# Expert blocks of the first four rows split off, and state-space fronts issued beside the other blocks

## The chip, the cores and the metric

The kernel runs on one core of one Trainium2 chip. The metric is the device time of one launch in microseconds (us). Before the change it is 3760.65 us, the median of three runs (3760.41 to 3761.23). Engines are named as in the profile: PE (TensorE matmul), PEld (TensorE weight load), DVE (VectorE), ACT (ScalarE), POOL (GpSimd) and SP (SyncE, which only issues DMAs here).

## The reference

The input x has 32 rows of 256 tokens of 128 floats. Two layers follow each other; each has a mixer and a feed-forward part, each with shift, scale and gate vectors per row from a modulation matmul. Layer 0 mixes by 16-head attention with rotary positions, then routes each token to two of eight gated experts. Layer 1 mixes by a state-space scan in both directions, followed by a sine and cosine expansion, and ends with capacity-limited experts. The change touches the experts of layer 0 and the start of the state-space part. Cut to these:

```python
# layer 0, experts: top-2 of 8, for every token of every row
logits = x @ gate_w
mult, sel = _sparse_mixer_routing(logits)              # two experts and their factors
w = jnp.sum(mult[:, :, None] * (sel[:, :, None] == jnp.arange(E)[None, None, :]), axis=1)
h = jax.nn.silu(jnp.einsum('th,ehf->etf', x, w1)) * jnp.einsum('th,ehf->etf', x, w3)
out = jnp.einsum('etf,efh,te->th', h, w2, w)
# layer 1, state space, for every row
xz = jnp.einsum('ble,ie->bli', x, in_w)
xc, z = jnp.split(xz, 2, axis=-1)
xc = _silu(conv(xc, conv_w) + conv_b)                  # 4 taps along the tokens
dt, Bm, Cm = jnp.split(jnp.einsum('bld,rd->blr', xc, xproj_w), [DTR, DTR + DS], axis=-1)
dt = jax.nn.softplus(jnp.einsum('blr,dr->bld', dt, dt_w) + dt_b)
h = dA_t * h + dBx_t                                   # scan over the tokens
```

## The kernel before, in words

The stages run one behind the other: modulation, attention, expert blocks of layer 0, state-space stage, experts of layer 1.

**Attention and routing.** Attention takes row after row in an order written out by hand (`with tc.manual_schedule`, L651): the engines PE, ACT, DVE and POOL execute what the loop issues, in that order. Behind attention, `routed` (L314) routes finished rows in chunks (`CHUNKS`, six of four rows, four of two). It normalizes and modulates the rows into h (L327 and L328 are its two POOL multiplications), multiplies by the gate, finds the two experts and their factors with small DVE operations, counts where each token stands in its expert's room (`filled` keeps the counts over chunks), and scatters each 128-token tile twice into `rows_in` by an indirect DMA on POOL (`scattered`, L276, issue at L280). `rows_in` has a room for all tokens per expert, plus one block; before the first scatter `blanked` (L242) fills it with blank rows, in four parts from a tile of 16 rows a partition, at rows 2 to 5 of attention. The last chunk (rows 30 and 31) is finished only when attention is, so its routing stands alone behind it (L781).

**Block table and blocks.** From `filled`, DVE works out for each block which expert and which rows it has (L785 to L822): blocks hold 256 rows of one expert, so 2·8192/256 + 8 − 1 = 71 blocks are enough for every split of the tokens. The loop at L826 then makes for each block: an indirect gather of the expert's weights (L830; skipped by an index out of bounds if its buffer, of three, has them already), an indirect gather of 256 rows (L839, five buffers), the cast of their targets (to_u, L847, DVE), two transposes (L850, PE, into PSUM of two buffers) and their copy (L852, DVE), the matmuls pa and pb in two halves (L861), Silu (L862, ACT), the product g (L863, DVE), the matmuls po (L869, eight of 128 columns for each token tile), the scaling (L877, ACT) and two scatters into `rows_out` (L280, POOL). Here no order is written out: a list scheduler orders the instructions by their dependences, and can move those of other parts ahead, as it does with the taps multiplication of `weights_kept` (L690, called at block 17, L828; its POOL operation is L700), the loads of the state-space weights.

**State-space stage.** Again an order by hand (L1347), in units g; a row has 16 of them (`UNITS`). Its `front` (L1005) is cut into 22 steps at the slots of `FRONT_AT`, from 39 units ahead of the row's first scan pass to 5 ahead. The front loads the row's two expert outputs (of_two, L1012, SP) and vectors gb and mod (L1014, L1016), adds them into x on POOL (L1018 to L1020), normalizes (L296 to L308: statistics on DVE, rstd on POOL, ACT), modulates (L1024, L1025), normalizes again, transposes (L157), and makes in_w (L1039), conv (L1053, four groups of eight matmuls), Silu (L1059), xp (L1069), the loads bc_d and bc (L1082), dt_w (L1096), Abs and Relu (L1103, L1104), Exp and Ln (L1106, L1107), and dt and u on POOL (L1109, L1111). All matmuls of fronts share one PSUM bank. ACT's function tables are loaded by hand in this stage (`table`, L990; load at L992). Each unit then has arg and ub matmuls (L1269), da (L1275, ACT), by_b (L1286, DVE), the scan (L1293, DVE), by_c (L1306, POOL) and gathered (L1325, PE). The loop starts at unit −39: row 0's front therefore runs ahead of the first scan, behind the last block.

Of the kernel before, what the change touches and what calls it, by code (L numbers as in the profile page):

```python
# [21 lines left out]
P = 128  # L22
# [47 lines left out]
def body(ctx: ExitStack, tc: tile.TileContext, a: dict, out: bass.AP):  # L70
# [155 lines left out]
    n_blocks = 2 * n_tok // BR + E - 1  # L226
# [11 lines left out]
    rows_out = scratch.tile([2 * n_tok, D], F32, tag="rows_out", name="rows_out")  # L238
    FILL = 16
    blank = rc.tile([P, FILL, WID], F32, tag="blank", name="blank")  # L240

    def blanked(part, parts):  # L242

        if part == 0:
            nc.gpsimd.memset(blank[:], 0.0)
            nc.gpsimd.memset(blank[:, :, D : D + 1], float(4 * n_tok))
        n = room // P // FILL // parts
        flat = rows_in[0:room, :].rearrange("(p a k) w -> p a (k w)", p=P, k=FILL)
        ins = nc.scalar.dma_start(
            flat[:, part * n : (part + 1) * n, :],  # L250
            blank[:].rearrange("p k w -> p (k w)").unsqueeze(1).to_broadcast([P, n, FILL * WID]),
        )
        blanks.append(ins.ins.name)
        if part == 0:
            nc.scalar.dma_start(rows_in[room:, :].rearrange("(p k) w -> p k w", k=2), blank[:, 0:2, :])
# [5 lines left out]
    nc.gpsimd.tensor_scalar(ids2[:], ids[:], float(n_tok), None, ALU.add)  # L261

    filled = rc.tile([P, E], F32, tag="filled", name="filled")
    nc.gpsimd.iota(
        filled[:], pattern=[[n_tok, E]], base=-1, channel_multiplier=0, allow_small_or_imprecise_dtypes=True
# [4 lines left out]
    groups = {"in": [], "out": []}  # L270
    sync = mybir.DependencyInfo(mybir.DependencyClass.Sync, mybir.DependencyReason.DATA)
    blanks = []
# [3 lines left out]
    def scattered(group, apart=False, **args):  # L276

        if apart:
            nc.gpsimd.memset(spacer[:], 0.0)
        ins = nc.gpsimd.indirect_dma_start(in_offset=None, **args).ins  # L280
        tc.declare_no_dep(ins, group=group, reason="rows of their own")
        tc.add_to_no_dep_group(group, ins)
        for b in blanks if group == "in" else ():
            tc.add_manual_dep(ins, b, sync, reason="blank rows first")
        groups[group].append(ins.name)
# [28 lines left out]
    def routed(first, n_rows, bank, apart):  # L314

        n = 2 * n_rows
        k = f"{n}_"
# [78 lines left out]
        for t in range(n):  # L396
            for row_u, h in zip(rows_at, hs):
                scattered(
                    "in",
                    apart,  # L400
                    out=rows_in[:],
# [4 lines left out]


    with ExitStack() as st:
# [8 lines left out]
        def a_bank():  # L417
            return ps_m.tile([P, 512], F32, tag="m", name="m")

# [231 lines left out]
        with tc.manual_schedule(engines=MANUAL):  # L651
            for s in range(-2 * UNITS_A - PREPARED, n_s + 9 * UNITS_A):
# [18 lines left out]
                if i == 2 and b - 2 in range(4):  # L671
                    blanked(b - 2, 4)
                last = b >= n_b - 1
                if i == (0 if last else 2) and b - 1 in starts[1:-1]:
                    c = starts.index(b - 1) - 1
                    behind.append(routed(starts[c], CHUNKS[c], a_bank, True))
# [5 lines left out]
                if s > n_s + UNITS_A + 1 and not streams and not behind:  # L682
                    break
# [6 lines left out]
    def weights_kept():  # L690
# [50 lines left out]


        das = [wc.tile([P, 4 * T + 1], F32, tag=f"da{i}", name=f"da{i}") for i in range(3)]
        for t in das:
            nc.gpsimd.memset(t[:, :: T], 0.0)

        behind = wc.tile([4 * DS, 1], F32, tag="behind", name="behind")
        nc.vector.tensor_copy(behind[:], ident[: 4 * DS, DTR : DTR + 1])
# [11 lines left out]


    with ExitStack() as st:
# [3 lines left out]
        ps_m = pool(st, "b_psm", 2, PSUM)  # L766
# [9 lines left out]
        empty = bc.tile([P, E], F32, tag="empty", name="empty")  # L776
        nc.gpsimd.iota(
            empty[:], pattern=[[n_tok, E]], base=-1, channel_multiplier=0, allow_small_or_imprecise_dtypes=True
        )

        for _ in routed(starts[-2], CHUNKS[-1], lambda: ps_m.tile([P, 512], F32, tag="m", name="m"), False):  # L781
            pass


        restart("k")  # L785
        blocks = thin(bc, E)
        nc.vector.tensor_tensor(blocks[:], filled[:], empty[:], ALU.subtract)
        nc.vector.tensor_scalar(blocks[:], blocks[:], 1.0 / BR, 0.5 - 0.5 / BR, ALU.mult, ALU.add)
        nc.vector.tensor_scalar(blocks[:], blocks[:], ROUND, None, ALU.add)
        nc.vector.tensor_scalar(blocks[:], blocks[:], -ROUND, None, ALU.add)  # L790
        upto = thin(bc, E)
        nc.vector.tensor_tensor_scan(upto[:], ones[:, :E], blocks[:], 0.0, ALU.mult, ALU.add)
        past = wide(bc, n_blocks)
        nc.vector.tensor_tensor(
            past[:],
            iota_k[:].unsqueeze(2).to_broadcast([P, n_blocks, E]),
            upto[:].unsqueeze(1).to_broadcast([P, n_blocks, E]),
            ALU.is_ge,
        )
        of = thin(bc, n_blocks)  # L800
        nc.vector.tensor_reduce(of[:], past[:], AX.X, ALU.add)
        nc.vector.tensor_tensor(past[:], past[:], blocks[:].unsqueeze(1).to_broadcast([P, n_blocks, E]), ALU.mult)
        at = thin(bc, n_blocks)
        nc.vector.tensor_reduce(at[:], past[:], AX.X, ALU.add)
        nc.vector.tensor_tensor(at[:], iota_k[:], at[:], ALU.subtract)
        nc.vector.tensor_scalar(at[:], at[:], float(P), None, ALU.mult)

        nc.vector.scalar_tensor_tensor(at[:], of[:], float(n_tok // 2), at[:], ALU.mult, ALU.add)
        nc.vector.tensor_scalar(at[:], at[:], float(room // 2), iota_p[:], ALU.min, ALU.add)
        at_u = bc.tile([P, n_blocks], U32, tag="at_u", name="at_u")  # L810
        nc.vector.tensor_copy(at_u[:], at[:])

        nc.vector.tensor_scalar(of[:], of[:], float(E - 1), float(P), ALU.min, ALU.mult)
        w_at = thin(bc, n_blocks)
        nc.vector.tensor_scalar(w_at[:], of[:], iota_p[:], None, ALU.add)
        same = thin(bc, n_blocks)
        nc.vector.tensor_tensor(same[:, WBUF:], of[:, WBUF:], of[:, : n_blocks - WBUF], ALU.is_equal)
        nc.vector.scalar_tensor_tensor(
            w_at[:, WBUF:], same[:, WBUF:], float(2 * E * P), w_at[:, WBUF:], ALU.mult, ALU.add
        )  # L820
        w_u = bc.tile([P, n_blocks], U32, tag="w_u", name="w_u")
        nc.vector.tensor_copy(w_u[:], w_at[:])  # L822

        ws = [bc.tile([P, ROW], F32, tag=f"w{i}", name=f"w{i}") for i in range(WBUF)]
        two_rows = rows_in[:].rearrange("(r k) w -> r (k w)", k=2)
        for j in range(n_blocks):  # L826
            if j == n_blocks // 4:
                weights_kept()  # L828
# [13 lines left out]
                in_=two_rows,  # L842
                in_offset=bass.IndirectOffsetOnAxis(ap=at_u[:, j : j + 1], axis=0),
            )
            reads("in", got)
# [20 lines left out]
            for t in range(2):  # L866
                for c in range(NF):
# [11 lines left out]
                    "out",  # L879
                    out=rows_out[:],  # L880
                    out_offset=bass.IndirectOffsetOnAxis(ap=to_u[:, t : t + 1], axis=0),
                    in_=o[:, t, :],
                    bounds_check=2 * n_tok - 1,
                    oob_is_err=False,
                )
    layer0.close()
# [79 lines left out]
    with ExitStack() as st:  # L966
        sp = pool(st, "c_sp", 2)
        one = pool(st, "c_one", 1)
# [4 lines left out]
        ps_m = pool(st, "c_psm", 1, PSUM)  # L973


        y_bank = ps_y.tile([P, 2, T], F32, tag="y", name="y")
        m_bank = ps_m.tile([P, 2 * T], F32, tag="m", name="m")

        def bank():
            return m_bank  # L980

# [609 lines left out]
```

## Time and profile before

The profile is of one execution on the chip. Its own time is 32 us above the median of the runs; differences are taken within it.

| what | us |
|---|---|
| median of the runs | 3760.65 |
| profiled execution, its time | 3792.99 |
| profiled execution, its span | 3791.0 |
| last attention matmul (L632) starts | 870.49 |
| first block matmul pa (L861) starts | 921.11 |
| last block matmul group po (L869) starts | 1361.47 |
| first scan pass (L1293) starts | 1425.63 |
| PE busy in the span | 3141.5 (83%) |
| POOL busy in the span | 2678.0 (71%) |

How to read it: every line of the profile has a start, a length, an engine and a source line; brackets hold the time for which the engine stood idle ahead of it, and what ended that. PEclk is the TensorE clock that was granted. "out<-in" are the program's own names.

### The profile page before, as it was taken

What the parts mean: (1) busy time and instruction counts of PE and PEld (TensorE: products, weight loads), DVE (VectorE), ACT (ScalarE), POOL (GpSimd) and SP (SyncE); (2) the same over time, 40 slices, a digit from 0 to 9 for tenths busy, and PEclk for the clock granted to TensorE, in tenths of its full rate; (3) what the DMA queues carried; (4) which work ended last, traced back from release to release, by engine and by line L of the source; (5) the groups of instructions that cost most, each with busy time, mean ns of one, the idle gap of its engine ahead of it and who ended that gap; (6) DMA issues with size and microseconds to landing.
All of it is one profiled execution on the core that took longest, in us unless ns stands there. A gap on an engine that the chain in (4) does not pass through costs nothing.

```text
span 3791.0 us, 69007 instructions
## 1 busy us (share of the span) xinstructions
PE 3141.5 (83%) x27464; PEld 2150.3 (57%) x27464; DVE 2620.6 (69%) x3526; ACT 2340.3 (62%) x3402; POOL 2678.0 (71%) x2724
## 2 busy tenths in 40 slices
PE   6999999884999968888888888888888888788854
PEld 3655655553888845555555555555555555555543
DVE  3666666643233319988888988888988888988942
ACT  3666666551333325777777677777677777777751
POOL 4466666645666647887887887888888888888842
PEclk8999999986999978988988888889888889889966
DMA  2720000002222211111111111111111111111102
GB/s 78 285 113 27 24 27 25 28 18 83 92 85 87 82 34 30 28 32 36 32 32 36 32 33 37 32 34 35 32 33 37 32 37 32 32 39 26 29 17 72
DMA packets 149686, 183.27 MB, mean 48 GB/s; under 512 B 31263, under 2 KB 112950, under 8 KB 145140
## 3 DMA queue, kind: packets, MB, share of 16 engines
q1 hardware_dynamic: 121892, 97.72, 11.1%
q0 software_dynamic: 23168, 46.93, 3.9%
q10 hardware_dynamic: 4304, 34.21, 2.2%
q8 instruction: 215, 3.52, 0.4%
q14 instruction: 107, 0.88, 0.1%
HBM read 130.24 MB, written 86.41 MB: 57 GB/s over the span
## 4 chain that ended last, share of the span: by engine, by line
POOL 22%; PE 18%; ACT 9%; issue 7%; DVE 7%; ACTq 1%; DMA 1%; POOLq 0%; SPq 0%; DVEq 0%
POOL hs L1306 11%; PE m L1180 5%; PE arg L1269 4%; POOL r L1162 3%; DVE hs L1293 3%; ACT da L1275 3%; PE y L1325 3%; ACT L992 3%; DVE ub L1286 2%; PE m L1133 1%; PE ub L1269 1%; PE y L1314 1%; POOL rstd L303 1%; ACT mag L1171 1%; ACT r L1170 1%
## 5 line engine op out<-in xcount | busy, mean ns | idle before, releaser
L1306 POOL TENSOR_TENSOR hs<-hs,bc 128x1024 f32<-128x1024 f32 x512 | 1204.7, 2363 | 342.1 <-DVE hs L1293 322.6
L1293 DVE TENSOR_TENSOR_SCAN hs<-da,ub 128x1024 f32<-128x1024 f32 x512 | 1167.3, 2280 | 31.7 <-POOL u L1111 0.5
L1269 PE MATMUL arg<-dt,spread_a 32*128 32x256 f32 x4096 | 718.6, 447 | 95.4 <-ACT da L1275 91.4
L1275 ACT ACTIVATE da<-arg 128x1020 f32<-128x1020 f32 x512 | 521.5, 1019 | 345.1 <-PE ub L1269 286.0
L1269 PE MATMUL ub<-u,spread 32*128 32x256 f32 x4096 | 670.3, 445 | 41.9 <-DVE hs L1293 41.7
L1286 DVE TENSOR_TENSOR ub<-ub,bc 128x1024 f32<-128x1024 f32 x512 | 620.7, 1212 | 108.5 <-PE ub L1269 108.5
L1269 PEld LDWEIGHTS arg<-dt,spread_a 32*128 32x128 f32 x4096 | 432.1, 207 | 287.7 <-ACT da L1275 171.1
L576 DVE TENSOR_REDUCE q<-x 128x4 f32<-128x1024 f32 x256 | 312.8, 1222 | 214.2 <-PE x L569 199.6
L1269 PEld LDWEIGHTS ub<-u,spread 32*128 32x128 f32 x4096 | 410.1, 207 | 70.5 <-DVE hs L1293 64.4
L572 ACT ACTIVATE ex<-e 128x1024 f32<-128x1024 f32 x256 | 261.9, 1023 | 204.5 <-PE x L569 178.1
L569 PE MATMUL e<-qmT,kqT 32*128 32x256 f32 x2048 | 343.6, 415 | 52.5 <-ACT ex L572 52.1
L1325 PE MATMUL y<-hs,gather 128*32 128x256 f32 x4096 | 338.4, 456 | 0.8 <-POOL hs L1306 0.8
L992 ACT ACT_TABLE_LOAD x257 | 329.7, 1283 | 5.2 <-PEq L1575 0.7
L569 PE MATMUL x<-kqT 32*128 32x256 f32 x2048 | 305.0, 415 | 10.5 <-DVE q L576 10.5
L569 PEld LDWEIGHTS e<-qmT,kqT 32*128 32x128 f32 x2048 | 217.5, 191 | 111.1 <-ACT ex L572 83.9
L1053 PE MATMUL m<-oT,taps 128*128 128x256 f32 (+3 forms) x1024 | 261.9, 400 | 6.9 <-DVE tots L929 3.5
L1180 PE MATMUL m<-coef,mag 128*128 128x128 f32 x1024 | 225.3, 304 | 47.2 <-DVE h L1188 30.9
L1053 PEld LDWEIGHTS m<-oT,taps 128*128 128x128 f32 x1024 | 189.5, 195 | 78.4 <-issue 48.5
L1180 PEld LDWEIGHTS m<-coef,mag 128*128 128x128 f32 x1024 | 167.7, 206 | 104.6 <-DVE h L1188 43.5
L280 POOL DMA_INDIRECT rows_out<-o,to_u x142 | 144.3, 1016 | 114.3 <-ACT o L877 91.6
L863 DVE TENSOR_TENSOR g<-g,pb 128x512 f32<-128x512 f32 x142 | 97.6, 688 | 165.2 <-PE pb L861 153.3
L1325 PEld LDWEIGHTS y<-hs,gather 128*32 128x32 f32 x4096 | 121.1, 124 | 158.3 <-issue 112.1
(332 smaller groups left out, 6227.9 us busy)
## 6 DMA issues: line engine op xcount, KB each, us to landing
rows_in<-blank ACTq DMA_DIRECT2D x4, 8320.0 KB, 24.9
bc_d<-xd SPq DMA_DIRECT2D x64, 256.0 KB, 5.3
bc<-bc_d SPq DMA_DIRECT2D x32, 512.0 KB, 3.7
of_two<-rows_out SPq DMA_DIRECT2D x64, 128.0 KB, 2.6
mod_b<-mod SPq DMA_DIRECT2D x32, 256.0 KB, 4.0
mod<-mod SPq DMA_DIRECT2D x32, 192.0 KB, 3.2
x<-in_x SPq DMA_DIRECT2D x16, 256.0 KB, 5.5
mod<-mod SPq DMA_DIRECT2D x32, 128.0 KB, 3.0
```

The source lines that it names most:

```text
L569: nc.tensor.matmul(to, lhs, rhs, start=True, stop=True)
L572: nc.scalar.activation(ex[:], exs[k_e][:], AF.Exp, scale=1.0 / math.sqrt(DH))
L576: nc.vector.tensor_reduce(pad("q", b)[:, :, 2 * i : 2 * i + 2, DH].rearrange("p t h -> p h t"), found[:], AX.X, ALU.max, negate=True,)
L992: nc.scalar.preload_act_table_set(which)
L1053: nc.tensor.matmul(to, taps[:, d, n, c, :], of, start=(s == 0), stop=(c == 0), skip_group_check=True)
L1180: nc.tensor.matmul(ps[:, t * D : (t + 1) * D], turned[k // (GRID // 2)][1 - j][:, k % (GRID // 2), t * P : (t + 1) * P], coef[:, j, k, :], ...
L1269: nc.tensor.matmul(to, lhs, rhs, start=True, stop=True)
L1275: nc.scalar.activation(e.da.rearrange("p (g t) -> p g t", t=T)[:, :, inner], e.arg[:].rearrange("p i j t -> p (i j) t")[:, :, inner], AF.Exp,)
L1286: nc.vector.tensor_tensor(by_four, by_four, b_of, ALU.mult)
L1293: nc.vector.tensor_tensor_scan(e.hs[:].rearrange("p g t -> p (g t)")[:, ::step], e.da[:, ::step], e.ub[:].rearrange("p i j t -> p (i j t)" ...
L1306: nc.gpsimd.tensor_tensor(e.hs[:], e.hs[:], c_of, ALU.mult)
L1325: nc.tensor.matmul(y[r * RG : (r + 1) * RG, :], gather[:, q, :], of.hs[:, 2 * j + p, :], start=False, stop=(q == NQ - 1), skip_group_check ...
```

## The change

Rows 0 to 3 (the first chunk) get rooms, outputs, counts and blocks of their own: `early_in`, `early_out`, `early_filled`, and 2·1024/256 + 7 = 15 early blocks; the other 28 rows keep `rows_in` and `rows_out` with 2·7168/256 + 7 = 63 blocks. The early blocks come directly behind attention. The routing of the last chunk no longer stands ahead of all blocks: after each early block two of its steps are issued. The table of the later blocks comes behind the early ones. The transposes of the blocks have one PSUM buffer in place of two, because the fronts' bank is now reserved from the end of attention on.

The fronts are taken out of the state-space stage, with a pool of their own (`c_fp`). A class `Lead` keeps their slots; `ahead.step()` issues the front steps of one unit. It is called after each later block from the 15th on, and what is left follows the last block; units −39 to −3 are issued this way: all of row 0's front, twelve steps of row 1's and three of row 2's. They have the list scheduler's order, as the blocks around them, and `table` does nothing there, so loads of ACT's tables are put in by the compiler where functions change. The state-space loop starts at unit −2. The tiles da, with their memset (L745 before), are made at the start of the state-space stage instead of in `weights_kept`.

In attention, early blank rows are written at row 2 and the four parts for `rows_in` at rows 3 to 6, from a tile in attention's own pool; the loop no longer ends only when the routing in it has ended. The rest is renaming and pools.

```diff
-    n_blocks = 2 * n_tok // BR + E - 1
+    n_early = CHUNKS[0] * T
+    early_blocks = 2 * n_early // BR + E - 1
+    n_blocks = 2 * (n_tok - n_early) // BR + E - 1
...
-    def routed(first, n_rows, bank, apart):
+    def routed(first, n_rows, bank, apart, rh, rt):
         n = 2 * n_rows
+        group, to_rows, filled = ("in", rows_in, later_filled) if first else ("early_in", early_in, early_filled)
...
-                if s > n_s + UNITS_A + 1 and not streams and not behind:
+                if s > n_s + UNITS_A + 1 and not streams:
                     break
...
+    fp = state_space.enter_context(tc.tile_pool(name="c_fp", bufs=2, side="right"))
+    ps_s = state_space.enter_context(tc.tile_pool(name="c_pss", bufs=1, space=PSUM, side="right"))
+    m_bank = ps_s.tile([P, 2 * T], F32, tag="m", name="m")
...
+        group, outs = ("out", rows_out) if b >= CHUNKS[0] else ("early_out", early_out)
         for i in range(2):
-                of_i = rows_out[i * n_tok + b * T : i * n_tok + (b + 1) * T, :]
-                reads("out", nc.sync.dma_start(of_two[:, i], of_i.rearrange("(t p) d -> p t d", p=P)))
+            at = i * outs.shape[0] // 2 + b * T
+            of_i = outs[at : at + T, :]
+            reads(group, nc.sync.dma_start(of_two[:, i], of_i.rearrange("(t p) d -> p t d", p=P)))
...
+    class Lead:
+        def step(self):
+            if self.at >= -2:
+                return False
+            self.begin(self.at)
+            self.steps(self.at)
+            self.steps(self.at + 0.5)
+            self.at += 1
+            return True
+    ahead = Lead()
...
-        for _ in routed(starts[-2], CHUNKS[-1], lambda: ps_m.tile([P, 512], F32, tag="m", name="m"), False):
-            pass
...
-        for j in range(n_blocks):
-            if j == n_blocks // 4:
-                weights_kept()
+        assert early_blocks % WBUF == 0
+        behind.append(routed(starts[-2], CHUNKS[-1], routing_bank, False, rh, rt))
+        where = block_table("j", early_blocks, early_filled, n_early)
+        for j in range(early_blocks):
+            block(j, where, "early_", early_in, early_out)
+            if j == 2:
+                weights_kept()
+            for _ in range(2):
+                if behind and next(behind[0], behind) is behind:
+                    behind.pop(0)
+        for steps in behind:
+            for _ in steps:
+                pass
+        where = block_table("k", n_blocks, later_filled, n_tok)
+        for j in range(n_blocks):
+            block(j, where, "", rows_in, rows_out)
+            if j >= n_blocks // 4:
+                ahead.step()
+        while ahead.step():
+            pass
...
-            for g in range(FRONT_AT[0], n_u + 6 * UNITS):
+            for g in range(ahead.at, n_u + 6 * UNITS):
```

## The prediction

> **What bounds the kernel now.** The page's forty slices come first: they show which engine is full in which stage. A slice is 94.8 us; attention is slices 1 to 9, the expert blocks are the end of slice 10 to the middle of slice 15, the state-space stage follows.
>
> ```profile
> PE   6999999884999968888888888888888888788854
> DVE  3666666643233319988888988888988888988942
> POOL 4466666645666647887887887888888888888842
> PEclk8999999986999978988988888889888889889966
> ```
>
> The reader is to see PE at nine tenths through the blocks (slices 11 to 14), and two dips of PE and of its clock, at slices 9 to 10 and 15: the two seams that the change works on. The windows of 10 us open them. Columns: window, length, then busy time (and count) of PE, PEld, DVE, ACT, POOL, then granted clock, DMA share, GB/s. The first fence is the seam ahead of the blocks, with the first blocks behind it, the second that behind them.
>
> ```profile
> 900.00:910.00 10.00, 0.00 (x0) 0.00 (x0) 8.28 (x28) 0.00 (x0) 7.33 (x9) 0.50 0.13 40
> 910.00:920.00 10.00, 1.32 (x4) 0.58 (x4) 1.09 (x4) 0.00 (x0) 6.24 (x7) 0.50 0.36 113
> 920.00:930.00 10.00, 8.89 (x36) 7.55 (x37) 1.59 (x5) 2.16 (x4) 3.23 (x4) 0.71 0.58 204
> ```
>
> ```profile
> 1370.00:1380.00 10.00, 0.00 (x0) 0.00 (x0) 1.41 (x8) 0.88 (x2) 5.41 (x11) 0.50 0.35 87
> ```
>
> At the first seam DVE and POOL work in turn (block table, eight row scatters) and PE does nothing. At the second one row's front runs as a chain with one engine at a time. The timeline gives the ends (start, length, engine, line; in brackets the idle time before it and what ended it).
>
> ```profile
> 888.39 1.18 POOL L328 TENSOR_TENSOR h<-h,mod 128x512 f32<-128x512 f32 x1
> 913.19 1.00 POOL L839 DMA_INDIRECT h<-rows_in,at_u  x1 [2.15 <-DMA rows_in<-h,4_row]
> 921.11 2.04 PE L861 MATMUL pa<-hT,w 128*128 128x256 f32 x4 [2.59 <-issue]
> ```
>
> ```profile
> 1361.47 1.16 PE L869 MATMUL po<-w,g 128*128 128x128 f32 x8 [0.51 <-ACT o L877]
> 1363.31 0.98 POOL L280 DMA_INDIRECT rows_out<-o,to_u  x1 [0.63 <-ACT o L877]
> 1380.86 0.86 PE L157 MATMUL m<-ident,o 128*128 128x128 f32 x2 [18.23 <-ACT o L308]
> 1425.63 2.29 DVE L1293 TENSOR_TENSOR_SCAN hs<-da,ub 128x1024 f32<-128x1024 f32 x1
> ```
>
> So 71 blocks last from 921.11 to 1362.63, 441.5 us, **6.2 us a block** (6.15 between Silus), and from the last po to the first scan pass 63.0 us. Who limits a block is in the waits of 925 to 1362 (total, times, longest):
>
> ```profile
> DVE to_u L847 <- DMA h<-rows_in,at_u: 110.5, 53, 3.6
> POOL rows_out L280 <- ACT o L877: 91.0, 68, 6.2
> PE po L869 <- DVE g L863: 24.7, 28, 1.4
> ```
>
> PE waits only 24.7 us in 437: blocks are PE's. But POOL issues four indirect DMAs a block (two scatters, one weight and one row gather), each 1.0 long with 0.3 before it: 5.3 us of 6.15, so it has 0.85 us to spare. And DVE, which works in order, sits at to_u until the row gather has landed, while g, which PE waits for, stands behind it. In the periods I read to_u ended 0.3 to 1.4 us before its g could start. A POOL that falls further behind stops PE.
>
> **The change, part by part**, against the profiled run (3792.99 us, span 3791.0; that is 32.3 above the 3760.65 median, so I carry the difference, not the time, over to the median).
>
> *First seam, saved.* The first blocks need only the scatters of rows 0 to 3, done long before. In the changed order of POOL the first row gather follows the routing's second multiplication (L328, ends 889.57) directly. So it starts near 889.6, the first weight gather at 890.9; the weight of before was issued at 915.77 and its first pa came 5.34 later, so pa starts near 896.5: **24.6 us saved**. What could be late next is the taps multiplication (L700, 4.93 us on POOL), now behind the third row gather; it ends near 901.5, before block 0 has rows to scatter: no cost.
>
> *Seven more blocks.* 2·1024/256+7 = 15 early and 2·7168/256+7 = 63 later are 78, not 71. 7 × 6.15 = **43.1 us**, all on PE's path.
>
> *The last routing between early blocks.* Its eight scatters took 10.1 us (900.94 to 911.05); POOL now issues them in one run behind the first scatter of block 5, ahead of that block's weight gather, its second scatter and the row gather five blocks on. With some 2 us for the casts that they wait for (0.46 and 2.15 are the waits at the old place, so 0 to 4) POOL loses 12.4 less the 1.4 that to_u had: **11 us**; 0 if the queue had a block in hand, 14 with the longer wait. The small DVE operations (two routing and table stretches, 5.8 and 8.3 us of DVE before) now stand between g multiplications. DVE is busy 3 of 10 us there, so most are hidden: **3 us**, from 0 to 8. The idle PE that they filled is already in the first term.
>
> *Fronts beside the later blocks.* All of row 0's front, twelve steps of row 1's and three of row 2's are issued there, from later block 15 in the program. The scheduler puts their POOL operations in front, between later blocks 1 and 8: of_two, gb and x (3 × 0.72 a row, three rows), four sets of rstd (1.4 each) and two of h (1.44), 15 us, and 3.4 us for the gaps and a fifth set: 18.4 over five blocks with 0.85 to spare each is **13 us** (18.4 − 4.3 − 1). At their old place they waited 0.83 for DVE, 1.88 for gb, 0.99 for ACT; if POOL sits these out in its queue, 9 us more. The two dt and u operations (2 × 2.34) come later, **4 us** (0 to 4.7). PE gets row 0's 4 in_w, 32 conv, 8 xp and 8 dt matmuls and 4 + 8 of row 1: 64 of 256 columns, each 0.217 us at full clock (four pa from 1197.69 to 1198.56), and two pairs of transposes, 14.4 us. As 24.7 us of PE's stalls are spread over the blocks, part goes into those: **9 us**, from 0 to 22 (one bank serves all, and the 0.66 us that PE waited for ACT between convs, twelve times, would add 8). SP's queue has slack everywhere here; its loads bc_d and bc (5.3 and 3.7) have blocks to hide in.
>
> *ACT tables.* Outside the hand-written stage the loads are put in as needed: eight more, for the routing's Exp and the front's Exp and Ln, between Silus. Row: 1.28 each, 10.3 us; ACT is busy 3.3 of 10 us, so half of it, **5 us** (0 to 10.3). A rule that speaks against the change: the Trainium skill, "ScalarE: Activation LUTs", section "What ACT_TABLE_LOAD costs", gives 1283 ns and about 1380 ns of drain for a switch. Here the load at 1399.03 is 1.28 long and the Silu behind it starts at 1400.33, 0.02 later, so the row shows no drain behind it; by the rule eight loads would be an estimated 21 us and the sum up to 11 more.
>
> *Second seam, saved.* Of the 63.0 us there remains, behind the last po at 1362.63: the o eviction and scatter to 1364.3, its landing (2.2, as for the row scatters at 913.19), the memsets of da's first columns that now stand there (0.17 for three), one da (1.02), one by_b and the scan's queue: 6.3. **56.7 us saved**; what is late next is that scatter and da. From the first scan on every slot is as before: 0.
>
> Sum: −24.6 − 56.7 + 43.1 + 11 + 3 + 13 + 4 + 9 + 5 = **+6.8 us**. 3760.65 + 6.8 ≈ **3767** (profiled 3800).
>
> What I leave at zero is the pace of the ordinary block. PSUM for the transposes falls from two buffers to one, and PE now has one block's transposes in every gap ahead of the second half of po, where before it had two blocks' in one and none in the next:
>
> ```profile
> 1201.37 0.71 PE L869 MATMUL po<-w,g 128*128 128x128 f32 x4 [0.91 <-DVE g L863]
> ...
> 1206.28 0.60 PE L850 MATMUL m<-ident,h 128*128 128x128 f32 x4
> ```
>
> The gap with transposes belongs to a period of 5.91 without a stall, the one without to 6.4 with 0.57 to 0.91 of it. Half the filling in each gap (0.3) leaves some 0.4 of stall each: 6.15 again. Bounds: 5.91 and 6.4, that is −19 to +20 us over 78 blocks.
>
> **Rivals.** (1) *Regular gaps.* If one block's transposes cover the wait for g, 78 × 0.24 = 19 us go, and the fronts' PE work, which then finds the same idle places, costs nothing (9 less): 3767 − 27 = **3740**, faster. For it: PE stalls on g are the only ones it has, and the front fills them; against: PE was 10.00 busy of 10 in some windows. With those 9 gone, it decides from a pace of 6.08 on (5.3 us over 78 blocks are then enough to pass −7.5). (2) *POOL becomes the bound*, the other side of no change: between later blocks 1 and 8 POOL, in order, sits out the front's answers (9 us) and gets no slack back (5.3 and 1.4), and PE waits for ACT between convs (8): 3767 + 24 = **3791**. For it: to_u's 110.5 us of waiting for POOL's gathers; it decides once POOL is more than 1.4 us behind. A PE that stalls also loses clock: in the window 990 to 1000 it had 0.87. (3) *It doesn't hide the fronts*: dt and u of row 0 come only behind the last block, because a read waits for all scatters. Then the second seam saves nothing, and the 13 + 4 + 9 fall away: 3767 + 57 − 26 = **3798**. Against it: the early blocks scatter to a tensor of their own.
>
> **Chances.** What this kernel's measurement can tell from no change is 0.2%, 7.5 us (3753.1 to 3768.2). The sum stands just inside that bound. Forecast as summed 0.45, own range 3751 to 3785 (of it faster 0.02, same 0.21, slower 0.22); rival 1 0.27, faster; rival 2 0.23 and rival 3 0.05, slower. Faster 0.29, same 0.21, slower 0.50. Both signs hold much, so the range reaches past rival 1 and rival 2 by some 5 and 14 us for the loose bounds of pace and queue: 3735 to 3805.
>
> **What will show it.** First pa near 896 to 897 and the last early block's end near 1003 (896.5 + 15 × 6.15 + 14); a gap in PE of about 10 us after early block 5 to 8; Silu to Silu over 6.5 at later blocks 1 to 8 and 6.15 after; first scan 6 to 7 us behind the last po; from there on the same length as before, 2365 us. A steady period under 6.0 makes rival 1 right, the gaps' sizes at blocks 1 to 8 rival 2, a front behind the last po rival 3. Wrong altogether would be a change of pace in attention, which the change touches only in where blank rows are written (the early rooms' 4.3 MB more, row parts one row later).

## The result, and the profile after

The changed kernel takes **3769.6 us** (median of twelve runs, 3761.9 to 3773.1) against 3761.1 for the kernel before in the same set of runs (3758.1 to 3769.6). The ratio is 1.0019, with a 95% interval of 1.0010 to 1.0028: 0.2% slower, 8.6 us. Predicted were 3767 and +6.8. The mechanism of the sum was right in most terms; one term that it left at zero was not zero, and the profile that it started from was not the kernel's usual one. Both are shown below.

The slices of the page of the changed kernel (94.2 us each):

```profile
PE   6988898876899998888888888888788888888864
DVE  3566666654323329888888988888988888988942
POOL 4466556556766657888888888888887887888852
PEclk6999999987999998999989888988888889888976
```

Of PE's two dips the first is shallower (slices 9 and 10 have 7 and 6 where 8 and 4 stood), and the second, slice 15 with 6, is gone. In the windows of 10 us (same columns as in the prediction) the first seam ends earlier: at 900 to 910 PE is busy for 9.65 us, where it had 0.00 before:

```profile
890.00:900.00 10.00, 0.83 (x3) 0.46 (x4) 0.59 (x2) 1.93 (x3) 8.11 (x8) 0.50 1.07 334
900.00:910.00 10.00, 9.65 (x44) 8.13 (x45) 6.66 (x11) 2.53 (x5) 8.01 (x8) 0.82 0.42 154
```

From the timeline, the first pa, and then the second seam:

```profile
899.86 2.04 PE L1072 MATMUL pa<-hT,w 128*128 128x256 f32 x4 [1.51 <-issue]
```

```profile
1405.05 1.16 PE L1080 MATMUL po<-w,g 128*128 128x128 f32 x8
1406.89 0.97 POOL L293 DMA_INDIRECT rows_out<-o,to_u  x1 [0.70 <-ACT o L1088]
1409.10 0.18 POOL L1218 MEMSET da<- 128x5 f32 x3 [1.24 <-DMA rows_out<-o,to_u]
1409.51 1.28 ACT L1365 ACT_TABLE_LOAD   x1 [2.90 <-DMA rows_out<-o,to_u]
1410.80 1.02 ACT L1365 ACTIVATE da<-arg 128x1020 f32<-128x1020 f32 x1
...
1411.88 0.62 PE L1359 MATMUL arg<-dt,spread_a 32*128 32x256 f32 x1 [3.12 <-ACT da L1365]
...
1414.13 1.23 DVE L1376 TENSOR_TENSOR ub<-ub,bc 128x1024 f32<-128x1024 f32 x1 [10.41 <-PE ub L1359]
...
1415.45 2.29 DVE L1383 TENSOR_TENSOR_SCAN hs<-da,ub 128x1024 f32<-128x1024 f32 x1
```

What stands between the last po and the first scan is now the landing of the last scatter (POOL's memset of da waits for it), a table load, da, the next arg and ub matmuls, which wait for da, and by_b (L1376): 9.2 us from the end of po at 1406.21, where 6.3 was forecast. The forecast had neither the table load (1.28) nor those matmuls (1411.88 to 1414.1).

The first profile of the kernel before cannot be subtracted from this one: its execution was 32 us over its median. The kernel before was therefore profiled once more (run e1). Lengths between landmarks, all from the timelines (last attention output matmul, first and last Silu of the blocks, first scan, last by_c in the window up to 3760, end of the span):

| stretch | before, first profile | before again (e1) | changed |
|---|---|---|---|
| to the last attention matmul | 870.5 | 874.5 | 873.4 |
| from there to the first Silu | 52.7 | 52.8 | 28.6 |
| first to last Silu of the blocks | 435.4 | 403.9 | 500.2 |
| from there to the first scan | 67.1 | 69.5 | 13.4 |
| first scan to the last by_c | 2213.8 | 2212.8 | 2208.2 |
| from there to the end | 151.6 | 148.7 | 143.1 |
| span | 3791.0 | 3762.1 | 3766.7 |

Two things are to be seen. The blocks hold what the first profile had too much: 435.4 against 403.9, 31.5 us, where the other stretches differ by −4.0 to +2.9 and the spans by 28.9. And against e1 the seams give back 80.3 us, and the blocks take 96.3 more.

### The profile page after: what moved, and what is told of

Read it like the earlier page. It is cut to its first block, busy times and chain, and to the rows that moved or that the text cites. A ratio compares the mean times of both kernels' runs of the same rounds, so it can differ in the third digit from the quotient of the medians.

```text
span 3766.7 us, 69781 instructions
## 1 busy us (share of the span) xinstructions
PE 3157.5 (84%) x27702; PEld 2176.9 (58%) x27702; DVE 2637.2 (70%) x3573; ACT 2360.9 (63%) x3437; POOL 2705.9 (72%) x2755
## 4 chain that ended last, share of the span: by engine, by line
PE 25%; POOL 22%; ACT 9%; issue 8%; DVE 7%; DMA 1%; POOLq 0%; SPq 0%; DVEq 0%; ACTq 0%
POOL hs L1396 11%; PE m L1273 5%; PE arg L1359 4%; DVE hs L1383 4%; POOL r L1255 3%; ACT da L1365 3%; PE y L1415 3%; ACT L799 3%; PE po L1080 2%; PE pa L1072 2%; PE pb L1072 2%; DVE ub L1376 2%; PE m L1226 1%; PE y L1404 1%; PE ub L1359 1%
## 5 line engine op out<-in xcount | busy, mean ns | idle before, releaser
L1383 DVE TENSOR_TENSOR_SCAN hs<-da,ub 128x1024 f32<-128x1024 f32 x512 | 1166.8, 2279 | 31.5 <-POOL u L923 0.5
L1359 PE MATMUL arg<-dt,spread_a 32*128 32x256 f32 x4096 | 710.6, 443 | 98.2 <-ACT da L1365 93.9
L1376 DVE TENSOR_TENSOR ub<-ub,bc 128x1024 f32<-128x1024 f32 x512 | 620.4, 1212 | 102.1 <-PE ub L1359 101.7
L1080 PE MATMUL po<-w,g 128*128 128x128 f32 x1248 | 188.6, 285 | 33.5 <-DVE g L1074 29.5
L1273 PE MATMUL m<-coef,r 128*128 128x128 f32 x1024 | 209.2, 288 | 0.0
```

What stands on the lines that cost most here:

```text
L1080: nc.tensor.matmul(po[:, t * D : (t + 1) * D], g[:, c, t * P : (t + 1) * P], w[:, f : f + D], start=(c == 0), stop=(c == NF - 1), skip_gro ...
L1273: nc.tensor.matmul(ps[:, t * D : (t + 1) * D], turned[k // (GRID // 2)][1 - j][:, k % (GRID // 2), t * P : (t + 1) * P], coef[:, j, k, :], ...
L1359: nc.tensor.matmul(to, lhs, rhs, start=True, stop=True)
L1376: nc.vector.tensor_tensor(by_four, by_four, b_of, ALU.mult)
L1383: nc.vector.tensor_tensor_scan(e.hs[:].rearrange("p g t -> p (g t)")[:, ::step], e.da[:, ::step], e.ub[:].rearrange("p i j t -> p (i j t)" ...
```

## The experiments

Times are medians. There were three sets of runs on three chips; every kernel is compared with the kernel before in its own set: 3760.6 (e1 to e4), 3798.8 (e5 to e8), 3761.9 (e9 to e12).

**e1: the kernel before again**, unchanged.

> The kernel before once more, unchanged, for a second profile: the first profiled execution (span 3791.0) lies 32 us over the median, and the changed kernel's (3766.7) lies at its own median, so their stages cannot be subtracted. Theory (costs of the blocks eat the saved seams): span near 3759; attention's last output matmul, first pa, last po, first scan at the same distances from each other as in the first profile (50.6 us, 441, 64) and the 32 us gone evenly or from the state-space stage. Rival (the loss lies outside the seams and blocks): attention or the state-space stage come out shorter than in the changed kernel by more than 5 us (870.5 against 873.4 at the last attention matmul, 2351 us from the first scan on).

Measured: one run of 3764.0, span 3762.1. The distances at the seams are the same to 2.5 us, and the excess of the first profile had been in the blocks, which the theory had expected to stay at 441. The rival falls too, as from the first scan on it takes 2361.5 and not less than the changed kernel's 2351.3. A Silu follows the one two halves before it after 5.91 and 5.48 us in turn, mean 5.70, where the first profile had 5.91 and 6.4. The gap behind the first half of po in e1's timeline, without and with transposes in it:

```profile
1159.73 0.61 PE L869 MATMUL po<-w,g 128*128 128x128 f32 x4
1160.17 0.60 PE L861 MATMUL pa<-hT,w 128*128 128x256 f32 x2
1160.74 0.71 PE L869 MATMUL po<-w,g 128*128 128x128 f32 x4
```

```profile
1154.26 0.60 PE L850 MATMUL m<-ident,h 128*128 128x128 f32 x4
1154.83 0.71 PE L869 MATMUL po<-w,g 128*128 128x128 f32 x4
```

Of PE's waits for g, 24.7 us in the prediction's profile, this one has (930 to 1335; total, times, longest):

```profile
PE po L869 <- DVE g L863: 1.9, 4, 1.0
```

Either way PE does not wait: the next block's pa fills the gap as well as two blocks' transposes do. In the first profile the same pa stood there (1199.86), but g came 0.9 later against it and PE waited 0.91. So the row on which the prediction built its pace was a disturbed period.

**e2: one PSUM bank for the transposes in the kernel before.**

```diff
-        ps_m = pool(st, "b_psm", 2, PSUM)
+        ps_m = pool(st, "b_psm", 1, PSUM)
```

> The kernel before with one thing of the change: the blocks' transposes have one PSUM buffer in place of two. Theory (regular gaps: one block's transposes ahead of every second half of po; in the changed kernel the undisturbed blocks keep 5.91 us, where before they alternate 5.91 and 6.4, mean 6.13): 71 x 0.22 = 15.6 us less, 3745 against 3761, with a period of 5.91 nearly throughout. Rival (the pace of the changed kernel comes from something else, such as the new weights' places or the fronts filling gaps, and one bank alone makes PE wait for the copy of the transposes): the period 6.13 or more, 3761 to 3780.

Measured: 3773.5, ratio 1.0031 (1.0020 to 1.0043): **slower by 12.9 us**. The period is 5.91 nearly throughout, as expected, but what it has to be held against is 5.70, not 6.13; the blocks take 418.4, which is 14.5 more than in e1. With one bank each gap holds one block's transposes (two in place of four), the next pa needs their copy, and PE waits for g in gap after gap:

```profile
1103.63 0.61 PE L869 MATMUL po<-w,g 128*128 128x128 f32 x4
1104.07 0.38 PE L850 MATMUL m<-ident,h 128*128 128x128 f32 x2
1104.64 0.71 PE L869 MATMUL po<-w,g 128*128 128x128 f32 x4 [0.19 <-DVE g L863]
```

The changed kernel has the same gap with the same wait:

```profile
1302.00 0.38 PE L1061 MATMUL m<-ident,h 128*128 128x128 f32 x2
1302.57 0.71 PE L1080 MATMUL po<-w,g 128*128 128x128 f32 x4 [0.19 <-DVE g L1074]
```

**e3: no calls of `ahead.step()`.**

```diff
-            if j >= n_blocks // 4:
-                ahead.step()
-        while ahead.step():
-            pass
```

> The changed kernel without its second half: no front step is issued beside the blocks, the state-space loop begins at unit -39 again, ahead of the first scan. Early blocks, one bank and the rest stay. Theory: the blocks lose their excess over 5.91 us at the front's POOL operations (17.2), convs (2.6) and dt and u (9.8), and the second seam comes back (67.1 less 13.4 from last Silu to first scan = 53.7): +24 us against the changed kernel, 3794. Rival (the fronts cost the blocks only their PE work, 14 us, and the rest of the excess belongs to early blocks and clock): +39, 3809.

Measured: 3767.8, ratio 1.0016 (1.0007 to 1.0025), the same as the changed kernel. Both theories fell: from last Silu to first scan it still takes 12.5 us, and the blocks 498.8. Row 0's front ran beside the blocks although its steps were now written in the hand-ordered stage behind them, as POOL's first front operation in this run's timeline shows:

```profile
1013.29 0.73 POOL L830 TENSOR_TENSOR of_two<-of_two 128x256 f32<-128x256 f32 x1
```

The scheduler moves it there as soon as its data allow it. The hand order fixes what stands behind what among its own instructions, and keeps nothing else from passing.

**e4: the last routing in hand order directly behind attention.**

```diff
-        behind.append(routed(starts[-2], CHUNKS[-1], routing_bank, False, rh, rt))
+        with tc.manual_schedule(engines=MANUAL):
+            for _ in routed(starts[-2], CHUNKS[-1], routing_bank, True, rh, rt):
+                pass
```

> The changed kernel with the last routing issued in hand order directly behind attention instead of two steps beside each early block; the first row and weight gathers still slip between its POOL operations, and its eight scatters stand ahead of block 0's scatters. Theory (the early blocks' excess of 15 us is the eight scatters that delay the weight gather of block 8 and the row gather of block 10, and DVE and table loads between): the first pa comes 4 us later (near 904), blocks 0 to 8 lose 10 of their 15 us of excess, -6 us against the changed kernel, 3763.5. Rival (the excess is the fifteen full weight gathers and the cold clock): the excess stays and the first pa is late, +4 to +10 us, 3774 to 3780.

Measured: 3769.9, ratio 1.0026 (1.0016 to 1.0036). The blocks lose 11.3 us (488.9), about as the theory had it, but the first Silu comes 13.3 later (41.9 behind attention in place of 28.6), as DVE's routing operations stand ahead of block 0's hT copy. (In this order a memset of one column stands between the scatters, as in attention.) So most of the early blocks' excess is the routing, not the weight gathers: of 15 us over the first nine periods 4 are left. That it costs about the same ahead of the blocks is in part chance, for 5.5 of the 13.3 us are one DVE operation, of 0.19 us at its next use (908.88), beside POOL's taps multiplication:

```profile
900.09 5.65 DVE L373 TENSOR_TENSOR 4_w<-4_w,4_w 128x32 f32<-128x32 f32 x1 [0.29 <-ACT 4_w L372]
900.77 4.92 POOL L726 TENSOR_TENSOR taps<-taps,in_w 128x512 f32<-128x512 f32 x4
```

It ends 0.05 us behind the multiplication, at 905.74.

**e5: fronts that wait for all scatters** (on e3).

```diff
-            reads(group, nc.sync.dma_start(of_two[:, i], ...))
+            got = nc.sync.dma_start(of_two[:, i], ...)
+            reads("early_out", got)
+            reads("out", got)
```

> The run without Lead's calls (e3) had its fronts beside the blocks all the same: the scheduler moved row 0's front out of the hand-ordered region. Here every load of of_two waits for all scatters, of early and later blocks, so no front can run before the last block; the rest as in e3. Theory (the gain of the second seam comes from the split of the tensors, not from where the steps are called, and the fronts cost the blocks 30 us): from last Silu to first scan 67 to 69 again in place of 12.5, the blocks lose 30 us of the 45 over 5.91 a block: +24 to +28 against the changed kernel, 3795. Rival (something else than the fronts disturbs the blocks at later blocks 3 to 6 and 29 to 33): the blocks stay at 499, +54, 3822.

Measured: 3811.2 against 3798.8, ratio 1.0033 (1.0021 to 1.0045). Last Silu to first scan 70.2, and the blocks 476.1, which is 24.1 less than in the changed kernel. Both parts of the theory hold within 6 us: hiding the fronts costs the blocks 24 us and gives 57. As the medians come from different sets, the spans are compared: 3808.0 against 3766.7, 41 us, of which 33 are these two terms; 6.6 lie behind the first scan, where the edit changes nothing.

**e6: inputs one block ahead** (one bank as in the change): `block` is split, and `block_in(j + 1)` with the gathers, the transposes and the hT copy is written ahead of `block(j)` with the matmuls.

```diff
+            if j + 1 < n_blocks:
+                block_in(j + 1, where, "", rows_in)
-            block(j, where, "", rows_in, rows_out)
+            block(j, "", rows_out)
```

> The changed kernel with the gathers, transposes and hT copy of a block written one block ahead of its matmuls, still with one PSUM bank for the transposes. On PE the next block's first pa matmul then stands between the transposes and the second half of po, which waits for g. Theory (the price of the one bank is that the next block's pa cannot fill the wait for g, 0.21 us a block: e2's 5.91 against 5.70 in the second profile of the kernel before): period 5.70, 78 x 0.21 = -16 us, 3753.5. Rival (5.91 is set by POOL's four indirect DMAs and the row gather behind them, or by the bank being written and read in turn): period stays 5.91, within 4 us of the changed kernel.

Measured: 3801.0 against 3798.8, ratio 1.0004 (0.9995 to 1.0013). Periods of 5.48 are there (pa again fills the gap), but between them stand others, mostly of 6.5 to 8, and the blocks take 527. Neither theory: the shorter period exists and is not kept. A period that was lost, in this run's timeline:

```profile
1213.12 0.60 PE L1078 MATMUL pa<-hT,w 128*128 128x256 f32 x2
1213.83 0.69 DVE L1080 TENSOR_TENSOR g<-g,pb 128x512 f32<-128x512 f32 x1 [1.53 <-PE m L1063]
1214.57 0.71 PE L1086 MATMUL po<-w,g 128*128 128x128 f32 x4 [0.85 <-DVE g L1080]
```

Here too the next pa stands in the gap, and g starts 1.5 us after its Silu had ended (1212.36), where it is 0.34 elsewhere. This gap looks like the lost ones of the first profile; that the cause is the same is not shown.

**e7: the sums of the fronts on DVE.**

```diff
+        first = nc.vector if b < 3 else nc.gpsimd
+        late = nc.vector if b < 1 else nc.gpsimd
-        nc.gpsimd.tensor_tensor(of_two[:, 0], of_two[:, 0], of_two[:, 1], ALU.add)
+        first.tensor_tensor(of_two[:, 0], of_two[:, 0], of_two[:, 1], ALU.add)
...
-        nc.gpsimd.tensor_tensor(dt[:], dt[:], u[:], ALU.add)
+        late.tensor_tensor(dt[:], dt[:], u[:], ALU.add)
```

> The changed kernel with the sums, products and modulation of the fronts of rows 0 to 2, and dt and u of row 0, on DVE in place of POOL; rstd stays on POOL. Theory (POOL is the bound where the fronts pass: 18.4 us of extra POOL work at later blocks 3 to 6, 4.7 at dt and u): the excess of 17 us at those blocks falls to 8, that of 10 at dt and u to 4: -13 to -15 us, 3755. Rival (PE's own front work, ACT's order and table loads make the excess): within 4 us of the changed kernel.

Measured: 3775.1 against 3798.8, ratio 0.9943 (0.9930 to 0.9957). The changed kernel was not in this set, so its 3755 has no direct measure; its blocks take 494.8, 5.4 less than in the changed kernel's profile and less gain than the 13 expected. In this set it is faster than the kernel before, by 24 us.

**e8: e6, e7 and da's tiles among the kept weights.**

```diff
-        das = [one.tile([P, 4 * T + 1], ...) for i in range(3)]   # start of the state-space stage
+        das = [wc.tile([P, 4 * T + 1], ...) for i in range(3)]    # in weights_kept
```

> The changed kernel with inputs one block ahead (e6), the fronts' sums on DVE (e7) and the tiles da with their memset back among the kept weights, so that da does not wait for the last scatter's landing. Theory: -16, -13 and -4 us add up but for some 5 us, as POOL has only 0.4 us a block to spare at a period of 5.70: -28, 3742, faster than the kernel before by 0.5%; from last po to first scan 5.3 in place of 9.2 us. Rival (the cuts are alternatives, as PE fills one stall or the other): about what e6 or e7 gives alone, 3753 to 3757.

Measured: 3786.9 against 3798.8, ratio 0.9969 (0.9956 to 0.9981), but 12 us more than e7 beside it: the irregular period of e6 again (blocks 513.2). The last part holds: last Silu to first scan is 9.5 in place of 13.4.

**e9: the changed kernel again.**

> The changed kernel once more, since the kernel before ran at 3761 in one set of runs and at 3799 in the other, and the changed one was only compared in the first. Theory (the kernel before has two paces of its blocks, 5.70 and 6.15 or more, as its POOL has 0.4 us a block to spare; the changed kernel has one, 5.91, in which POOL has 0.6): the changed kernel takes 3770 to 3785 whichever of the two the kernel before shows: ratio 1.002 against 3761, 0.995 against 3799. Rival (the second set of runs was slower for all kernels alike): 1.002 again in either.

Measured: 3772.1 against 3761.9, ratio 1.0025 (1.0016 to 1.0034). The kernel before showed its fast pace in this set, so the question of the other set was not answered directly. Against the rival speak e5 to e8, which ran in that set: attention (872.7 to 875.3 to its last matmul) and the stretch from the first scan on (2356.8 to 2361.8) are as long there as in the other sets (870.5 to 875.9, 2347.8 to 2365.4), and e5 and e7 keep the period of 5.91. Blocks 500.0, seams 28.4 and 13.1, as in the first profile of the changed kernel.

**e10: e7 and da's tiles kept, without e6.**

> The changed kernel with the fronts' sums on DVE (as e7) and da's tiles kept from the block stage on (as in e8); one bank and its period of 5.91 stay. Theory (e7 cut the excess at later blocks 3 to 6 from 17 to 8; the wait for the last scatter's landing is 4 us of the second seam, 13.4 to 9.5 in e8): -9 to -13 us against the changed kernel of the same set. Rival (what DVE takes over comes back as waits of g for DVE): within 4 us.

Measured: 3758.7 against 3761.9, ratio 0.9990 (0.9981 to 0.9999), and 13.4 us under e9. The blocks take 485.7 (14.3 less), the second seam 9.5 (3.5 less). The windows where the fronts' POOL work passes, of the changed kernel in e9, and of e10:

```profile
1030.00:1040.00 10.00, 8.09 (x29) 6.76 (x28) 2.00 (x7) 3.44 (x8) 8.79 (x14) 0.66 0.21 59
1040.00:1050.00 10.00, 5.59 (x28) 4.81 (x29) 2.39 (x10) 1.98 (x5) 7.29 (x13) 0.88 0.15 41
```

```profile
1030.00:1040.00 10.00, 9.30 (x60) 8.39 (x61) 4.46 (x16) 4.11 (x9) 7.89 (x13) 1.00 0.14 41
1040.00:1050.00 10.00, 8.82 (x52) 7.70 (x51) 2.63 (x6) 3.38 (x7) 7.58 (x8) 1.00 0.24 58
```

POOL's column (fifth) falls little, PE's (first) rises from 8.09 and 5.59 to 9.30 and 8.82, and its clock is no longer lost (0.66 and 0.88). Ten microseconds earlier, at 1020 to 1030, PE has less in e10 (6.26 against 7.62); over 1010 to 1050 it has 32.24 against 29.26 of 40, and POOL 29.76 against 32.68.

**e12: e10 with the last routing's scatters spread.** Each scatter waits for an eviction of its own block; the steps go four beside each of the first three early blocks, then one.

```diff
+        for name in held if group == "in" else ():
+            tc.add_manual_dep(ins, name, sync, reason="beside this block")
...
+            held[:] = outs_done[-1:]
-            for _ in range(2):
+            for _ in range(4 if j < 3 else 1):
```

> As e10, and the last routing's steps go four beside each of the first three early blocks, then one; each of its eight scatters waits for an eviction of its own block, so that POOL issues one a block in blocks 4 to 11 and not eight behind the scatter of block 5. Theory (the 15 us of excess in the early blocks is POOL held for 10 us in one place: at 1.3 a block against 0.6 to spare, 5 of them are lost): -6 to -9 us against e10. Rival (the routing's small DVE operations and table loads make the excess, and four steps at a time make it worse): 0 to +5.

Measured: 3756.0, ratio **0.9984** (0.9975 to 0.9993): the fastest kernel of the study, 6 us under the kernel before. Against e10 it is 2.7 us, not 6 to 9: the blocks that carry a scatter take 6.2 to 7.2, and the second period of the run took 11.6, as four steps at once stand in its way. POOL in the changed kernel, with the scatters of rows_in in one run, and in e12:

```profile
947.33 0.97 POOL L293 DMA_INDIRECT rows_in<-h,4_row  x1 [0.30 <-issue]
948.60 0.97 POOL L293 DMA_INDIRECT rows_in<-h,4_row  x1 [0.30 <-issue]
...
952.43 0.97 POOL L293 DMA_INDIRECT rows_in<-h,4_row  x1 [0.31 <-issue]
953.71 1.03 POOL L1041 DMA_INDIRECT w<-in_moe,w_u  x1 [0.30 <-DMA rows_in<-h,4_row]
```

```profile
941.52 0.97 POOL L294 DMA_INDIRECT rows_in<-h,4_row  x1 [0.30 <-DVE g L1086]
942.80 0.99 POOL L1062 DMA_INDIRECT h<-early_in,at_u  x1 [0.31 <-issue]
944.10 1.01 POOL L294 DMA_INDIRECT early_out<-o,to_u  x1 [0.30 <-issue]
945.41 1.04 POOL L1053 DMA_INDIRECT w<-in_moe,w_u  x1 [0.30 <-issue]
946.76 1.01 POOL L294 DMA_INDIRECT early_out<-o,to_u  x1 [0.31 <-issue]
948.07 0.97 POOL L294 DMA_INDIRECT rows_in<-h,4_row  x1 [0.30 <-issue]
```

In e12 POOL goes from one issue to the next in 1.31 us, five to a block, without a wait: 948.07 − 941.52 = 6.55, and the blocks' period there is 6.54. POOL goes on like this from 932 to 982: here it is the bound.

**e11: seven more blocks in the kernel before** (blank ones, which scatter nothing).

```diff
-    n_blocks = 2 * n_tok // BR + E - 1
+    n_blocks = 2 * n_tok // BR + E - 1 + 7
```

> The kernel before with 78 blocks in place of 71: the seven more are blank, gather blank rows and scatter nothing, but issue all their instructions; nothing else of the change. This prices the largest cost of the sum by itself. Theory: seven times the pace that the kernel before has in this set, +40 us at 5.70, +43 to +46 at 6.15 or more. Rival (blank blocks are cheaper, as their scatters move nothing and their weights are there): under +30.

Measured: 3792.7, ratio 1.0083 (1.0067 to 1.0098): +30.8 us. In its profile the blocks take 444.6, 40.8 more than in e1, or 5.8 a block: in the block stage blank blocks cost as others do. But the spans differ by 29.0 only, and the medians by 30.8, close to the rival's 30. The rest lies ahead of the blocks (2.4), in the seam behind them (67.0 against 69.5) and in the last stretch (142.3 against 148.7), which the edit does not touch; e1's one execution is also 3.4 over the median of its set.

## Why the prediction was right, and where it was not

The sum against what the runs gave, each from the blocks' length or a seam:

| step | predicted | measured | from |
|---|---|---|---|
| first seam saved | −24.6 | −24.2 | e1 and changed |
| second seam saved | −56.7 | −56.1 | e1 and changed |
| seven more blocks | +43.1 | +40.8 | e11 |
| last routing between blocks: 11, 3 and half of the tables | +16.5 | +15 | first nine periods, 68.1 − 9 × 5.91 |
| fronts: 13, 4, 9 and half of the tables | +28.5 | +24.1 | e5 and changed |
| pace of the ordinary block | 0 (−19 to +20) | +16 | e2: 14.5 for 71 blocks, scaled to 78 |
| sum | +6.8 | +15.6 | |

**Right** were the two seams, the seven blocks, the routing's run of scatters behind block 5's first scatter, and the place and the total of the fronts' cost: Silu to Silu 8.19, 15.21, 9.49 and 7.92 where POOL has the sums, and 12.44 where it has dt and u (6.81 in e10, with both on DVE; 6.1 us by e10 against e9, where 4 were forecast). A period of 10.25 shortly before is ACT's: two table loads and Exp stand between its Silus, it is 10.25 in e7 and e10 too, and short periods behind it give most of it back. The second seam came out right partly by luck, as 2.9 us more remained of it than forecast and the seam of e1 was 2.4 longer than that of the first profile. **Rival 3** was excluded as argued: the early blocks' own tensors let the fronts start; e3 and e5 show that this alone does it, and the calls between the blocks do nothing that the scheduler does not do.

**Wrong was the step "What I leave at zero is the pace of the ordinary block".** It said that half the filling in each gap leaves "6.15 again", from a profile whose gaps had a stall that is hardly there in e1 and e11 (PE's waits for g are 1.9 us in e1, not 24.7). The regular gap has 5.91, as rival 1 said, but the kernel before has 5.70 in e1 and e11, which are within 0.1% of their medians, so the single bank costs 0.21 a block and does not give 0.24. Rival 1 had the period and the evenness right and the sign wrong, and one block's transposes do not quite cover the wait for g: 0.19 us is left in a gap. The bound of +20 covered the size, though it stood for a pace of 6.4, which no run shows as the rule.

The measured terms sum to +15.6 and the blocks and seams of the two profiles to +16.0, while the medians differ by 8.6 and the two spans by 4.6. The rest, 11.4 in the spans, is in attention (1.1), from the first scan to the last by_c (4.6) and in the last stretch (5.6). The last stretch is the same work in all kernels and took from 142.3 (e11) to 151.6, and the changed kernel's second profile (e9) has 2212.2 from the first scan to the last by_c, close to e1's 2212.8, so neither is put down to the change. With the medians of e11 and e2 (+30.8 and, for 78 blocks, +14.2) in place of their profiles the terms sum to +3.8; the measured 8.6 lies between the two sums. That the forecast came out within 3 us of the measured median is thus partly luck: a term of +16 was missing, and some −7 to −11 against it lie in stretches that differ as much between executions.

The forecast of POOL as what carries the fronts' cost holds in part. Moving the sums to DVE took 14.3 of the blocks' 24.1 in e10 against e9, in one set, but 5.4 in e7 against the changed kernel, across sets; what made e7's blocks longer was not tried. At the ordinary pace POOL is not the bound: in e1, at 5.70, to_u waits longer for its gathers (over 930 to 1335, below) than in the first profile at 6.15 (110.5), and PE loses next to nothing by it.

```profile
DVE to_u L847 <- DMA h<-rows_in,at_u: 171.9, 66, 4.9
```

What stays open is why the stages of blocks whose gap holds the next pa (the kernel before, e6, e8) run at 5.48 and 5.91 in some executions and lose 0.6 us and more per gap in others, while those with only transposes there (the changed kernel, e2 to e5, e7, e9, e10, e12) kept 5.91 as their ordinary period in every profile, on every chip. In the lost gaps g starts late though Silu and pb are recorded as done. In the first profile PE loses over 0.3 us behind such a pa in 22 gaps; in 18 of them g starts 0.08 to 0.18 us behind the end of that pa, as if it waited for it. In e6 and e8 it mostly does not, and what holds it is not in the records. It decides the sign: where the kernel before takes 3799, e7 is 24 us faster than it; the changed kernel itself was not run there.

For the table loads, the Trainium skill's page "ScalarE: Activation LUTs" ("What ACT_TABLE_LOAD costs") gives some 1380 ns of drain beside the load. The changed kernel's loads between blocks do not show it either:

```profile
1202.86 1.28 ACT L918 ACT_TABLE_LOAD   x1
1204.16 1.06 ACT L918 ACTIVATE u<-u 128x1024 f32<-128x1024 f32 x1
```

Exp starts 0.02 us after the load has ended; the measurement decides, and the load is 1.28 us.

## What to carry to other kernels

Before a stage's pace goes into a sum, hold the profiled execution against the median, and if they differ, find the stage that holds the difference: here 31.5 us sat in one stage and turned the sign of a term. Splitting work off in order to start something earlier has to pay for the rounding of its blocks (41 us here) and for whatever it takes from the pipeline it runs beside, such as one PSUM bank (16 us). Small work that is put beside a full loop costs what its engine lacks there: here it cost less on the engine with room (DVE at 3 of 10, not POOL at 7 of 10).

## What the runs showed of the hardware that was not expected

One kernel can run its blocks at two paces: the kernel before took 403.9 and 435.4 us for them in two profiles, with the granted clock at 0.99 over the blocks of both. Its medians were 3761 to 3762 in three sets of runs and 3799 in a fourth; that the fourth had the slower pace is likely, but no profile of it was taken there. Indirect DMAs issue from POOL every 1.31 us (five in 6.55 us, e12), whether they scatter or gather rows or weights. A PSUM bank that was taken away from the transposes cost 0.19 us of wait in a gap of PE (e2), where the next block's matmul could no longer stand. And a short DVE operation can be held until a POOL multiplication ends: in every profile of the changed kernel and its variants but e4 the cast to_u of a first block takes 2.2 to 3.9 us in place of 0.17 and ends 0.02 to 0.04 us behind the taps multiplication (in e4 it is L373, above); the prediction had put taps at no cost.
